# Bias network recorded in text order ahead of the null key and value, its norm's factor moved into later steps

## The chip, the cores and the metric

The kernel runs on one core of a Trainium2 chip, in one launch. A core has five instruction streams that work side by side and wait for each other through semaphores: TensorE (PE, matmul and transpose), VectorE (DVE), ScalarE (ACT), GpSimd (POOL) and SyncE (SP, which issues DMAs); ACT issues some DMAs too. Each stream takes its instructions in the order in which they stand. The metric is the device time of the program in microseconds (us); less is better. Times in the trace are counted from the start of its span.

## The reference, cut to what matters

A batch of 8 sequences of 512 tokens and 256 channels goes through a conditioned attention, a delta-rule mixer and two mixtures of experts, all in float32. The change lies in what is prepared once for the attention: the relative position bias, and the part of the keys and values that belongs to the null key.

```python
def rel_pos_bias(n, w0, b0, g0, w1, b1, g1, w2, b2, dtype):
    pos = jnp.arange(-n + 1, n, dtype=dtype)[:, None]
    h = jax.nn.silu(ln(pos @ w0 + b0, g0))
    h = jax.nn.silu(ln(h @ w1 + b1, g1))
    h = h @ w2 + b2
    ...
    bias = h[idx]                       # idx = i - j + n - 1, one value for each head and distance
    return jnp.transpose(bias, (2, 0, 1))
```

Here `ln` subtracts the mean, divides by the root of variance plus 1e-5 and multiplies by a gain. The network has two hidden layers of 256 channels and ends in 16 heads. Attention is causal, so 512 positions are enough. The null key and value are one more column of the scores: `cond[0]` and `cond[1]`, the key normed and scaled by q_scale and k_scale.

## The kernel before, in words

`attention_setup` (from L142) loads the weights, runs the bias network, prepares the null key and value, and spreads the bias. After it comes one long order of steps (`attention_plan`, from L595): a row of score groups, and with every other piece of work due at a step number (`at(w.first - 14, attention_keys, s)`). `a.run(end)` records all steps up to `end`. Setup calls it three times: `a.run(-27)` (the first load of x), `a.run(-4)` after the null key (statistics, norm, turn, keys and queries of the first sequence), and the rest after setup.

The order on an engine is set by two things. Instructions recorded through `Ordered` or `a.mm` and `a.turn` keep the order of the program among themselves; those called straight on `nc` are placed by a scheduler that may move them past others. Before the change, SP's DMAs, the planned steps on DVE and ACT, and matmuls and turns of the plan keep program order; the whole setup calls `nc` directly and is woven between them, and POOL is free throughout.

The bias network works on four tiles of 128 positions. `act_T` (L208) is its step for one tile: mean and variance (`bn_stats` as_nst, `bn_aggr` as_nmv), plus eps, power -0.5 on POOL (as_nr, L101), subtract and multiply (L114), multiply by the gain (L211), tanh of half (L213), (tanh + 1) times h (L214), two turns on TensorE (as_tp, L217) and a copy from PSUM with factor 0.5 (as_h1T, as_h2T, L218). The first layer's h is position times w0 plus b0 (L224), the second's a matmul with w1 (as_hp, L229) plus b1 (L233). The last matmul with w2 gives as_gp (L237), DVE makes as_gs of it (L240), and SP writes it to DRAM as as_gd.

The null key: as_nrow and as_rk on DVE, a power on POOL, then for each of two halves as_wn on POOL (L257) and a sum on DVE into a_wkv's last 16 columns (L263). a_kp, the matmul of the keys (L131), reads a_wkv. The null value: as_nvb is cleared on POOL (L279) and filled by two copies on DVE (L280, L281), and eight matmuls with Wout make as_vps (L284), which is copied to a_vw.

Spreading the bias: for each of the 16 heads a DMA (half of them issued by SP, half by ACT) reads as_gd with shifted rows into as_hk (four buffers), one matmul with a flipped identity, called a flip here, makes as_bp (L274, two PSUM buffers), and ACT copies it into a_bias (L275). The first score group's a_bm (L450, POOL: bias plus mask row) reuses the room of setup's tiles, and so waits until they have been read.

The planned steps that lie beside this for the first sequence: statistics of x (a_st, a_mv), the norm's factors on POOL (a_nr, a_nmr), the mask row (a_mrow, L342), norm on ACT (a_x), turns (a_tp) and their copies (a_xnT), keys (a_kp, a_kv, a_k, a_rk, a_kn), their turn (a_ktp), then four half tiles of queries (a_qp, a_q, a_rq, a_sn on POOL, a_qtp). A matmul in float32 shows as two rows in the trace (two passes).

Of the kernel before, what the change touches and what calls it, by code (L numbers as in the profile page):

```python
# [18 lines left out]
P = 128  # L19
B, S, D = 8, 512, 256  # L20
NT = S // P
NCT = D // P
H1, DH = 16, 64
# [3 lines left out]
BIG = 1.0e30  # L27
# [114 lines left out]
def attention_setup(g, ctx, asides):  # L142
# [16 lines left out]
    with tc.tile_pool(name="as_c", bufs=1) as sp, tc.tile_pool(name="as_w", bufs=2) as wk, tc.tile_pool(  # L159
        name="as_ps", bufs=2, space=PSUM  # L160
    ) as ps:

        rows = {}
        for name in ("w0", "b0", "g0"):
            rows[name] = sp.tile([P, D], F32, name="as_" + name)
            src = ins["c_" + name]
            row_bc(a, rows[name], src[0] if name == "w0" else src)
        w1 = sp.tile([P, NCT, D], F32, name="as_w1")
        nc.scalar.dma_start(out=w1, in_=ins["c_w1"].rearrange(by_k, p=P))
        for name in ("b1", "g1"):  # L170
            rows[name] = sp.tile([P, D], F32, name="as_" + name)
            row_bc(a, rows[name], ins["c_" + name])
        w2 = sp.tile([P, NCT, H1], F32, name="as_w2")
        nc.scalar.dma_start(out=w2, in_=ins["c_w2"].rearrange(by_k, p=P))
        attention_plan(g, a, asides)
        a.run(-27)
        a.wkv = wp.tile([P, NCT, KVW], F32, name="a_wkv")
        a.sync.dma_start(out=a.wkv[:, :, 0 : 2 * DH], in_=ins["c_Wkv"].rearrange(by_k, p=P))
        a.wq = wp.tile([P, NCT, H1 * DH], F32, name="a_wq")
        a.sync.dma_start(out=a.wq, in_=ins["c_Wq"].rearrange(by_k, p=P))  # L180
        nrow = sp.tile([P, 4, DH], F32, name="as_nrow")
        row_bc(a, nrow[:, 0, :], ins["cond"][0])
        row_bc(a, nrow[:, 1, :], ins["c_q_scale"])
        row_bc(a, nrow[:, 2, :], ins["c_k_scale"])
        a.gn = wp.tile([P, NCT], F32, name="a_gn")
        nc.scalar.dma_start(out=a.gn, in_=ins["c_g_norm"].rearrange("(c p) -> p c", p=P))
        sc = sp.tile([P, 2], F32, name="as_sc")
        for i in range(2):
            hs = slice(i * DH, (i + 1) * DH)
            a.sync.dma_start(out=sc[hs, 0:1], in_=ins["c_q_scale"].unsqueeze(1))  # L190
            a.sync.dma_start(out=sc[hs, 1:2], in_=ins["c_k_scale"].unsqueeze(1))
        b2 = sp.tile([H1, 1], F32, name="as_b2")
        a.sync.dma_start(out=b2, in_=ins["c_b2"].unsqueeze(1))
        a.nab = wp.tile([P, H1], F32, name="a_nab")
        row_bc(a, a.nab, ins["c_null_attn_bias"])
        a.wout = wp.tile([P, 8, D], F32, name="a_wout")
        nc.scalar.dma_start(out=a.wout, in_=ins["c_Wout"].rearrange(by_k, p=P))
        nv = sp.tile([P, 1], F32, name="as_nv")
        a.sync.dma_start(out=nv[0:DH], in_=ins["cond"][1].unsqueeze(1))
        a.sync.dma_start(out=nv[DH:P], in_=ins["cond"][1].unsqueeze(1))  # L200
        a.go = wp.tile([P, NCT], F32, name="a_go")
        a.sync.dma_start(out=a.go, in_=ins["c_g_out"].rearrange("(c p) -> p c", p=P))


        h1T = sp.tile([P, NCT, S], F32, name="as_h1T")
        h2T = sp.tile([P, NCT, S], F32, name="as_h2T")

        def act_T(out, t, h, gain):  # L208
            hn = wk.tile([P, D], F32, tag="hn", name="as_hn")
            normalized(g, wk, hn, h, "as_n")  # L210
            nc.vector.tensor_mul(hn, hn, gain)  # L211
            th = wk.tile([P, D], F32, tag="th", name="as_th")
            nc.scalar.activation(th, hn, AF.Tanh, scale=0.5)  # L213
            nc.vector.scalar_tensor_tensor(hn, th, 1.0, hn, ALU.add, ALU.mult)  # L214
            tp = ps.tile([P, 512], F32, tag="tp", name="as_tp")
            for c in range(NCT):
                nc.tensor.transpose(tp[:, c * P : (c + 1) * P], hn[:, c * P : (c + 1) * P], g.ident)  # L217
            nc.scalar.activation(  # L218
                out[:, :, t * P : (t + 1) * P], tp[:, 0 : NCT * P].rearrange("p (c m) -> p c m", c=NCT), AF.Copy, scale=0.5
            )  # L220

        for t in range(NT):
            h = wk.tile([P, D], F32, tag="h", name="as_h")
            nc.vector.scalar_tensor_tensor(h, rows["w0"], g.pos[:, t : t + 1], rows["b0"], ALU.mult, ALU.add)  # L224
            act_T(h1T, t, h, rows["g0"])
        for t in range(NT):
            hp = ps.tile([P, 512], F32, tag="ps", name="as_hp")
            for c in range(NCT):
                nc.tensor.matmul(  # L229
                    hp[:, 0:D], h1T[:, c, t * P : (t + 1) * P], w1[:, c, :], start=c == 0, stop=c == NCT - 1  # L230
                )
            h = wk.tile([P, D], F32, tag="h", name="as_h2")
            nc.vector.tensor_add(h, hp[:, 0:D], rows["b1"])  # L233
            act_T(h2T, t, h, rows["g1"])
        gp = ps.tile([P, 512], F32, tag="ps", name="as_gp")
        for c in range(NCT):
            nc.tensor.matmul(gp[0:H1, :], w2[:, c, :], h2T[:, c, :], start=c == 0, stop=c == NCT - 1)  # L237
        gs = sp.tile([H1, S + P], F32, name="as_gs")
        nc.gpsimd.memset(gs[:, S:], BIG)
        nc.vector.tensor_scalar(gs[:, 0:S], gp[0:H1, :], b2, -1.0, ALU.add, ALU.mult)  # L240
        gd = g.dram.tile([H1, S + P], F32, name="as_gd")
        a.sync.dma_start(out=gd, in_=gs)


        nc.vector.tensor_scalar(a.ks, sc[:, 0:1], sc[:, 1:2], -8.0, ALU.mult, ALU.mult)

        rk = sp.tile([P, 1], F32, name="as_rk")
        nc.vector.tensor_mul(nrow[:, 3, :], nrow[:, 0, :], nrow[:, 0, :])
        nc.vector.tensor_reduce(rk, nrow[:, 3, :], AX.X, ALU.add)
        nc.vector.tensor_scalar(rk, rk, 1e-24, None, ALU.max)  # L250
        rsqrt(g, rk, rk)
        nc.vector.tensor_mul(nrow[:, 3, :], nrow[:, 1, :], nrow[:, 2, :])
        nc.vector.tensor_mul(nrow[:, 3, :], nrow[:, 3, :], nrow[:, 0, :])
        nc.vector.tensor_scalar(nrow[:, 3, :], nrow[:, 3, :], rk, -8.0, ALU.mult, ALU.mult)
        wn = sp.tile([P, H1, DH], F32, name="as_wn")
        for c in range(NCT):
            nc.gpsimd.tensor_tensor(  # L257
                wn,
                a.wq[:, c, :].rearrange("p (h d) -> p h d", h=H1),
                nrow[:, 3, :].unsqueeze(1).to_broadcast([P, H1, DH]),  # L260
                ALU.mult,
            )
            nc.vector.tensor_reduce(a.wkv[:, c, 2 * DH : KVW], wn, AX.X, ALU.add)  # L263

        a.run(-4)


        for h in range(H1):
            hk = wk.tile([P, S], F32, tag="hk", name="as_hk", bufs=4)
            row = gd[h]  # L270
            eng = a.sync if h % 2 else nc.scalar
            eng.dma_start(out=hk, in_=bass.AP(tensor=row.tensor, offset=row.offset, ap=[[1, P], [1, S]]))
            bp = ps.tile([P, 512], F32, tag="tp", name="as_bp")
            nc.tensor.matmul(bp, g.flip, hk, start=True, stop=True)  # L274
            nc.scalar.copy(a.bias[:, h, :], bp)  # L275


        nvb = sp.tile([P, 8 * H1], F32, name="as_nvb")
        nc.gpsimd.memset(nvb, 0.0)  # L279
        nc.vector.tensor_copy(nvb[0:DH, 0 : 8 * H1 : H1 + 2], nv[0:DH, 0:1].to_broadcast([DH, 8]))  # L280
        nc.vector.tensor_copy(nvb[DH:P, 1 : 8 * H1 : H1 + 2], nv[DH:P, 0:1].to_broadcast([DH, 8]))  # L281
        vps = ps.tile([P, 512], F32, tag="ps", name="as_vps")
        for c in range(8):
            nc.tensor.matmul(  # L284
                vps[0:H1, 0:D], nvb[:, c * H1 : (c + 1) * H1], a.wout[:, c, :], start=c == 0, stop=c == 7
            )
        nc.vector.tensor_copy(a.vw, vps[0:H1, 0:D])

    a.pp = ctx.enter_context(tc.tile_pool(name="a_pp", bufs=4))
    a.tr = ctx.enter_context(tc.tile_pool(name="a_tr", bufs=2, space=PSUM))  # L290
    a.av = ctx.enter_context(tc.tile_pool(name="a_av", bufs=2, space=PSUM))
# [1736 lines left out]
```

## Time and profile before

| | us |
|---|---|
| three runs: median (lowest, highest) | 2495.55 (2490.47, 2503.61) |
| the profiled execution, whole | 2498.42 |
| its span in the profile | 2496.6 |
| busy in the span: PE, DVE, ACT, POOL | 2336.8, 1422.1, 970.2, 1129.5 |
| bias network: first h, as_gp, as_gs | 7.64, 40.38, 44.01 |
| null key: first as_nrow, last a_wkv over | 19.02, 35.78 |
| the first a_kp, the other seven | 46.46, 47.44 |
| as_vps, the null value's matmuls | 44.70 to 51.68 |
| first and last flip (as_bp) | 52.65, 85.08 over |
| first a_bm | 85.16 |

The last lines are starts in the trace unless they say otherwise. The whole setup is the first 85 us of 2497. A row of the timeline gives start, length (of a merged row: from the first start to the last end), engine, line, operation, output and inputs, and in brackets how long the engine was idle before it and what ended that. The chain of waits is followed back from the last instruction of the span; its rows give start, length, and what the time went to.

### The profile page before, as it was taken

Reading aid. Unit: us, or ns where it says so; the run is one execution under the profiler, and the core shown is the slowest. Engines: PE = TensorE matmul, PEld = TensorE weight load, DVE = VectorE, ACT = ScalarE, POOL = GpSimd, SP = SyncE. Lnnn points to the kernel's source line nnn. Section 1 sums busy time; section 2 is a strip of 40 time slices with the busy share of each in tenths; the row PEclk is TensorE's granted clock in tenths of the full one; section 3 lists DMA queues with packets and bytes.
Section 4 is the critical chain, followed back from the end, with each engine's and each line's share of the span. In section 5 each row is a group of like instructions: output and inputs, shape, how many; then the busy total and the mean of one; then the engine's idle time right before and its main releaser. Section 6 shows DMA issues by size and latency. Waiting matters only on the chain.

```text
span 2496.6 us, 57237 instructions
## 1 busy us (share of the span) xinstructions
PE 2336.8 (94%) x22836; PEld 1726.3 (69%) x22836; DVE 1422.1 (57%) x3974; ACT 970.2 (39%) x2650; POOL 1129.5 (45%) x1427
## 2 busy tenths in 40 slices
PE   4899999999999995779899999999999999999998
PEld 2456565556655653456778787887887888888886
DVE  4466657676675775445647457466466467444333
ACT  2666767566666652322222223223222322211111
POOL 3677867767787651333324324225224234232211
PEclk7999999999999997768999999999999999999999
DMA  3201012011110014011323323334225134232433
GB/s 99 60 19 39 28 36 59 22 37 40 35 32 27 23 52 117 2 31 49 78 74 100 83 77 104 77 84 117 66 79 122 50 95 112 72 108 76 115 95 88
DMA packets 345179, 167.25 MB, mean 67 GB/s; under 512 B 193280, under 2 KB 323072, under 8 KB 344912
## 3 DMA queue, kind: packets, MB, share of 16 engines
q1 hardware_dynamic: 341904, 160.16, 23.9%
q8 instruction: 180, 2.95, 0.5%
q10 hardware_dynamic: 3008, 3.43, 0.5%
q14 instruction: 87, 0.71, 0.1%
HBM read 148.33 MB, written 15.18 MB: 65 GB/s over the span
## 4 chain that ended last, share of the span: by engine, by line
PE 76%; DVE 11%; POOL 5%; DMA 3%; ACT 2%; issue 2%; SPq 1%; ACTq 0%; DVEq 0%; POOLq 0%
PE m_guf L131 13%; PE m_gue L131 9%; PE m_accf L131 6%; PE a_op L131 6%; PE a_s L131 5%; PE a_av L131 4%; PE a_qp L131 4%; PE m_acce L131 4%; PE a_ptp L132 4%; PE d_pp L131 3%; PE d_op L131 2%; PE m_lp L131 2%; POOL a_bm L450 1%; DVE d_y L125 1%; PE d_cop L131 1%
## 5 line engine op out<-in xcount | busy, mean ns | idle before, releaser
L450 POOL TENSOR_TENSOR a_bm<-a_bias,a_mrow 128x1024 f32<-128x1024 f32 (+1 forms) x176 | 381.9, 2171 | 81.6 <-DVE a_mn L125 69.0
L131 PE MATMUL m_guf<-m_oute,m_wf 128*128 128x256 f32 x1536 | 379.8, 392 | 3.2 <-ACT m_oute L125 2.0
L131 PEld LDWEIGHTS m_guf<-m_oute,m_wf 128*128 128x128 f32 x1536 | 292.2, 195 | 56.3 <-issue 8.4
L131 PE MATMUL m_gue<-m_xT,m_we 128*128 128x256 f32 x1280 | 311.5, 386 | 11.4 <-DVE m_he L125 10.1
L125 DVE CUSTOM_DVE_ANT_0 a_pr<-a_s,a_bm,a_sn 128x512 f32<-128x512 f32 (+3 forms) x512 | 254.4, 546 | 66.1 <-PE a_s L131 51.0
L125 ACT ACTIVATE a_pr<-a_pr,a_mn 128x512 f32<-128x512 f32 (+3 forms) x512 | 282.0, 553 | 16.3 <-DVE a_mn L125 15.6
L131 PEld LDWEIGHTS m_gue<-m_xT,m_we 128*128 128x128 f32 x1280 | 236.8, 191 | 49.0 <-DVE m_he L125 14.2
L125 POOL TENSOR_TENSOR m_hf<-m_hf,m_ctf 128x256 f32<-128x256 f32 x128 | 97.0, 759 | 381.7 <-DVE m_hf L125 211.7
L125 DVE SCALAR_TENSOR_TENSOR m_tf<-m_tf,m_guf 128x256 f32<-128x256 f32 x192 | 80.5, 419 | 301.2 <-ACT m_tf L125 300.8
L125 ACT ACTIVATE m_tf<-m_guf 128x256 f32<-128x256 f32 x192 | 73.5, 383 | 373.9 <-PE m_guf L131 369.5
L125 POOL TENSOR_TENSOR m_he<-m_he,m_cte 128x256 f32<-128x256 f32 x128 | 105.1, 821 | 223.7 <-DVE m_he L125 121.1
L131 PE MATMUL a_s<-a_kT,a_qT 64*128 64x384 f32 (+3 forms) x1024 | 199.8, 471 | 6.7 <-DVE a_mn L125 6.4
L131 PE MATMUL m_accf<-m_hf,m_wf 128*128 128x256 f32 x768 | 200.1, 384 | 6.0 <-POOL m_hf L125 6.0
L125 DVE TENSOR_TENSOR m_te<-m_gue,m_te 128x256 f32<-128x256 f32 x160 | 67.7, 423 | 230.2 <-ACT m_te L125 230.2
L132 PE MATMUL a_ptp<-table,a_pr 128*128 128x128 f32 x1280 | 179.6, 278 | 19.7 <-DVE a_pT L125 18.2
L132 PEld LDWEIGHTS a_ptp<-table,a_pr 128*128 128x128 f32 x1280 | 145.5, 142 | 76.0 <-issue 29.5
L125 ACT ACTIVATE m_te<-m_gue 128x256 f32<-128x256 f32 x160 | 61.3, 383 | 290.8 <-PE m_gue L131 276.9
L131 PE MATMUL a_av<-a_pT,a_kv 128*64 128x256 f32 (+1 forms) x1216 | 165.1, 402 | 3.1 <-DVE a_pT L125 3.0
L131 PEld LDWEIGHTS m_accf<-m_hf,m_wf 128*128 128x128 f32 x768 | 148.1, 193 | 28.0 <-POOL m_hf L125 7.2
L131 PE MATMUL m_acce<-m_he,m_we 128*128 128x256 f32 x640 | 163.8, 381 | 0.0
L131 PEld LDWEIGHTS a_s<-a_kT,a_qT 64*128 64x128 f32 x1024 | 83.6, 186 | 80.1 <-issue 39.9
L131 PEld LDWEIGHTS m_acce<-m_he,m_we 128*128 128x128 f32 x640 | 121.6, 191 | 17.0
(350 smaller groups left out, 4169.2 us busy)
## 6 DMA issues: line engine op xcount, KB each, us to landing
a_rep<-a_rd SPq DMA_DIRECT2D x128, 128.0 KB
m_cte<-m_combe SPq DMA_DIRECT2D x64, 256.0 KB
m_ctf<-m_combf SPq DMA_DIRECT2D x128, 128.0 KB
m_we<-in_e_w_gate_dram SPq DMA_DIRECT2D x64, 128.0 KB
m_we<-in_e_w_up_dram SPq DMA_DIRECT2D x64, 128.0 KB
m_we<-in_e_w_down_dram SPq DMA_DIRECT2D x64, 128.0 KB
m_wf<-in_f_gate_w_dram SPq DMA_DIRECT2D x128, 64.0 KB
m_wf<-in_f_up_w_dram SPq DMA_DIRECT2D x128, 64.0 KB
```

The costliest lines, as they stand in the source:

```text
L125: return lambda *args, **kw: tc.keep_in_program_order(f(*args, **kw))
L131: mm = lambda *args, **kw: tc.keep_in_program_order(pe.matmul(*args, **kw))
L132: turn = lambda *args: tc.keep_in_program_order(pe.transpose(*args))
L450: nc.gpsimd.tensor_tensor(bm, a.bias[:, 2 * c0 : 2 * (c0 + pairs), (NT - 1 - t) * P :], s.mrow[:, 0:n].unsqueeze(1).to_broadcast([P, 2 * p ...
```

## The change

The network is recorded in text order. POOL is wrapped in `Ordered` for the length of setup, and DVE, ACT and TensorE use the plan's ordered handles; the null key's and null value's POOL and DVE instructions do the same (as_vps and the flips still call `nc`). The network stands first, then `a.run(-16)`, which records the first sequence's statistics, norm and turn, then the null key, then `a.run(-4)`. The memsets of as_gs and as_nvb, which the scheduler had put at the start of POOL's order, now stand where the text has them.

Within the network the work of a tile is cut into `first`/`second`, `centred` and `silu`, recorded a piece apart for neighbouring tiles. The norm's factor r is no longer multiplied into h. POOL makes x.r from 4 times the variance plus 4e-5, so x.r is half the old factor; tanh takes it as its scale; the first layer's output goes without it through w1 and gets it in the second layer's bias step (y.r); the second layer's output gets it in a copy on ACT (`last`). For each tile and layer the step for eps and one of two passes over h on DVE are gone, and POOL has one small instruction more. In all, DVE has 16 instructions fewer in the changed program, POOL 8 more and ACT 4 more.

In the changed program's order on TensorE, as_vps is split: two of its eight matmuls stand between the seventh and the eighth flip, two between later flips, and four behind the last one, ahead of the first scores. The load of ACT's function table waits for the first `centred` tile; before it waited for nothing. From the second score group on, every engine's order is that of before.

```diff
+        a.nc.gpsimd = Ordered(tc, nc.gpsimd)
+        v, act, pool = a.nc.vector, a.nc.scalar, a.nc.gpsimd
...
+        def summed(x, gain):
+            x.gain = gain
+            st = wk.tile([P, 6], F32, tag="as_nst", name="as_nst", bufs=4)
+            v.bn_stats(st, x.h)
+            x.mv = wk.tile([P, 2], F32, tag="as_nmv", name="as_nmv", bufs=4)
+            v.bn_aggr(x.mv, st)
+            x.r = wk.tile([P, 1], F32, tag="as_nr", name="as_nr", bufs=8)
+            pool.tensor_scalar(x.r, x.mv[:, 1:2], 4.0, 4e-5, ALU.mult, ALU.add)
+            pool.tensor_tensor(x.r, x.r, g.nhalf, ALU.pow)
+
+        def first(t):
+            x = layers[0][t]
+            x.h = wk.tile([P, D], F32, tag="h", name="as_h", bufs=4)
+            v.scalar_tensor_tensor(x.h, rows["w0"], g.pos[:, t : t + 1], rows["b0"], ALU.mult, ALU.add)
+            summed(x, rows["g0"])
+
+        def second(t):
+            y, x = layers[0][t], layers[1][t]
+            hp = ps.tile([P, 512], F32, tag="ps", name="as_hp")
+            for c in range(NCT):
+                a.mm(hp[:, 0:D], h1T[:, c, t * P : (t + 1) * P], w1[:, c, :], start=c == 0, stop=c == NCT - 1)
+            x.h = wk.tile([P, D], F32, tag="h", name="as_h2", bufs=4)
+            v.scalar_tensor_tensor(x.h, hp[:, 0:D], y.r, rows["b1"], ALU.mult, ALU.add)
+            summed(x, rows["g1"])
+
+        def centred(x):
+            v.scalar_tensor_tensor(x.h, x.h, x.mv[:, 0:1], x.gain, ALU.subtract, ALU.mult)
+            x.th = wk.tile([P, D], F32, tag="th", name="as_th", bufs=2)
+            act.activation(x.th, x.h, AF.Tanh, scale=x.r)
+
+        def silu(x, out, last):
+            v.scalar_tensor_tensor(x.h, x.th, 1.0, x.h, ALU.add, ALU.mult)
+            if last:
+                act.activation(x.h, x.h, AF.Copy, scale=x.r)
             tp = ps.tile([P, 512], F32, tag="tp", name="as_tp")
             for c in range(NCT):
-                nc.tensor.transpose(tp[:, c * P : (c + 1) * P], hn[:, c * P : (c + 1) * P], g.ident)
-            nc.scalar.activation(
-                out[:, :, t * P : (t + 1) * P], tp[:, 0 : NCT * P].rearrange("p (c m) -> p c m", c=NCT), AF.Copy, scale=0.5
-            )
+                a.turn(tp[:, c * P : (c + 1) * P], x.h[:, c * P : (c + 1) * P], g.ident)
+            act.copy(out[:, :, x.t * P : (x.t + 1) * P], tp[:, 0 : NCT * P].rearrange("p (c m) -> p c m", c=NCT))
 
         for t in range(NT):
...
+            first(t)
+        for t in range(NT + 1):
+            if t < NT:
+                centred(layers[0][t])
+            if t > 0:
+                silu(layers[0][t - 1], h1T, False)
+        for t in range(NT + 2):
+            if t < NT:
+                second(t)
+            if 0 < t <= NT:
+                centred(layers[1][t - 1])
+            if t > 1:
+                silu(layers[1][t - 2], h2T, True)
         gp = ps.tile([P, 512], F32, tag="ps", name="as_gp")
...
-        nc.gpsimd.memset(gs[:, S:], BIG)
-        nc.vector.tensor_scalar(gs[:, 0:S], gp[0:H1, :], b2, -1.0, ALU.add, ALU.mult)
+        pool.memset(gs[:, S:], BIG)
+        v.tensor_scalar(gs[:, 0:S], gp[0:H1, :], b2, -1.0, ALU.add, ALU.mult)
         gd = g.dram.tile([H1, S + P], F32, name="as_gd")
         a.sync.dma_start(out=gd, in_=gs)
+        a.run(-16)
...
-        rsqrt(g, rk, rk)
+        pool.tensor_tensor(rk, rk, g.nhalf, ALU.pow)
...
         for c in range(NCT):
-            nc.gpsimd.tensor_tensor(
+            pool.tensor_tensor(
                 wn,
...
-            nc.vector.tensor_reduce(a.wkv[:, c, 2 * DH : KVW], wn, AX.X, ALU.add)
+            v.tensor_reduce(a.wkv[:, c, 2 * DH : KVW], wn, AX.X, ALU.add)
 
         a.run(-4)
...
         nvb = sp.tile([P, 8 * H1], F32, name="as_nvb")
-        nc.gpsimd.memset(nvb, 0.0)
-        nc.vector.tensor_copy(nvb[0:DH, 0 : 8 * H1 : H1 + 2], nv[0:DH, 0:1].to_broadcast([DH, 8]))
-        nc.vector.tensor_copy(nvb[DH:P, 1 : 8 * H1 : H1 + 2], nv[DH:P, 0:1].to_broadcast([DH, 8]))
+        pool.memset(nvb, 0.0)
+        v.tensor_copy(nvb[0:DH, 0 : 8 * H1 : H1 + 2], nv[0:DH, 0:1].to_broadcast([DH, 8]))
+        v.tensor_copy(nvb[DH:P, 1 : 8 * H1 : H1 + 2], nv[DH:P, 0:1].to_broadcast([DH, 8]))
...
+    a.nc.gpsimd = nc.gpsimd
```

More of the change, by code (lines that the diff above doesn't have):

```diff
@@ L202, in attention_setup @@
         a.sync.dma_start(out=a.go, in_=ins["c_g_out"].rearrange("(c p) -> p c", p=P))
+        a.nc.gpsimd = Ordered(tc, nc.gpsimd)
+        v, act, pool = a.nc.vector, a.nc.scalar, a.nc.gpsimd
         h1T = sp.tile([P, NCT, S], F32, name="as_h1T")
         h2T = sp.tile([P, NCT, S], F32, name="as_h2T")
[L208 to L214, printed above, removed]
+        layers = [[SimpleNamespace(t=t) for t in range(NT)] for _ in range(2)]
@@ L222, in attention_setup @@
         for t in range(NT):
[L223 to L234, printed above, removed]
+            first(t)
@@ L235, in attention_setup @@
+        for t in range(NT + 1):
[10 more added lines that the diff above has]
+                silu(layers[1][t - 2], h2T, True)
         gp = ps.tile([P, 512], F32, tag="ps", name="as_gp")
         for c in range(NCT):
-            nc.tensor.matmul(gp[0:H1, :], w2[:, c, :], h2T[:, c, :], start=c == 0, stop=c == NCT - 1)
+            a.mm(gp[0:H1, :], w2[:, c, :], h2T[:, c, :], start=c == 0, stop=c == NCT - 1)
@@ L238, in attention_setup @@
         gs = sp.tile([H1, S + P], F32, name="as_gs")
-        nc.gpsimd.memset(gs[:, S:], BIG)
-        nc.vector.tensor_scalar(gs[:, 0:S], gp[0:H1, :], b2, -1.0, ALU.add, ALU.mult)
+        pool.memset(gs[:, S:], BIG)
+        v.tensor_scalar(gs[:, 0:S], gp[0:H1, :], b2, -1.0, ALU.add, ALU.mult)
         gd = g.dram.tile([H1, S + P], F32, name="as_gd")
         a.sync.dma_start(out=gd, in_=gs)
-        nc.vector.tensor_scalar(a.ks, sc[:, 0:1], sc[:, 1:2], -8.0, ALU.mult, ALU.mult)
+        a.run(-16)
@@ L247, in attention_setup @@
+        v.tensor_scalar(a.ks, sc[:, 0:1], sc[:, 1:2], -8.0, ALU.mult, ALU.mult)
         rk = sp.tile([P, 1], F32, name="as_rk")
-        nc.vector.tensor_mul(nrow[:, 3, :], nrow[:, 0, :], nrow[:, 0, :])
-        nc.vector.tensor_reduce(rk, nrow[:, 3, :], AX.X, ALU.add)
-        nc.vector.tensor_scalar(rk, rk, 1e-24, None, ALU.max)
-        rsqrt(g, rk, rk)
-        nc.vector.tensor_mul(nrow[:, 3, :], nrow[:, 1, :], nrow[:, 2, :])
-        nc.vector.tensor_mul(nrow[:, 3, :], nrow[:, 3, :], nrow[:, 0, :])
@@ L254, in attention_setup @@
-        nc.vector.tensor_scalar(nrow[:, 3, :], nrow[:, 3, :], rk, -8.0, ALU.mult, ALU.mult)
+        v.tensor_mul(nrow[:, 3, :], nrow[:, 0, :], nrow[:, 0, :])
+        v.tensor_reduce(rk, nrow[:, 3, :], AX.X, ALU.add)
+        v.tensor_scalar(rk, rk, 1e-24, None, ALU.max)
+        pool.tensor_tensor(rk, rk, g.nhalf, ALU.pow)
+        v.tensor_mul(nrow[:, 3, :], nrow[:, 1, :], nrow[:, 2, :])
+        v.tensor_mul(nrow[:, 3, :], nrow[:, 3, :], nrow[:, 0, :])
+        v.tensor_scalar(nrow[:, 3, :], nrow[:, 3, :], rk, -8.0, ALU.mult, ALU.mult)
@@ L286, in attention_setup @@
             )
-        nc.vector.tensor_copy(a.vw, vps[0:H1, 0:D])
+        v.tensor_copy(a.vw, vps[0:H1, 0:D])
+    a.nc.gpsimd = nc.gpsimd
     a.pp = ctx.enter_context(tc.tile_pool(name="a_pp", bufs=4))
```

## The prediction

> **What bounds the kernel now.** The page gives TensorE 94% of the span, but the change touches only the setup, so I read the chain of waits over the first 140 us, then the timeline of that stretch, then the windows table for the clock. The chain:
>
> ```profile
> 40.38 3.59 PE as_gp L237 x4
> ...
> 55.79 1.11 PE a_ktp L132 x4
> 56.90 9.31 PE a_qp L131 x16
> ...
> 68.72 2.68 PE as_bp L274 x6
> 71.42 3.81 DMA as_hk<-as_gd
> ...
> 85.16 6.99 POOL a_bm L450 x3
> ```
>
> The end of setup is one event, POOL's first a_bm at 85.16. The timeline says what it waited for, and gives the rows that I use below (start, length, engine, instruction, idle time before and its releaser):
>
> ```profile
> 23.07 2.40 POOL L257 TENSOR_TENSOR as_wn<-a_wq,as_nrow 128x1024 f32<-128x1024 f32 x1 [2.39 <-DVE as_nrow L254]
> ...
> 34.59 1.19 DVE L263 TENSOR_REDUCE a_wkv<-as_wn 128x16 f32<-128x1024 f32 x1
> ...
> 44.01 0.74 DVE L240 TENSOR_SCALAR as_gs<-as_gp,as_b 16x512 f32<-16x512 f32 x1 [4.29 <-PE as_gp L237]
> ...
> 47.44 1.98 PE L131 MATMUL a_kp<-a_wkv,a_xnT 128*128 128x144 f32 x14
> ...
> 52.54 1.93 POOL L342 TENSOR_SCALAR a_mrow<-a_mk 128x512 f32<-128x512 uint8 x1
> ```
> ```profile
> 73.41 0.22 POOL L422 TENSOR_TENSOR a_sn<-a_sn,a_nab 128x16 f32<-128x16 f32 x1
> ...
> 85.16 6.99 POOL L450 TENSOR_TENSOR a_bm<-a_bias,a_mrow 128x1024 f32<-128x1024 f32 x3 [11.54 <-PE as_bp L274]
> ```
>
> The reader is to see that a_bm waits for the sixteenth flip (as_bp), not for arithmetic; that the null key's work (as_wn, a_wkv) was over by 35.8, inside the network's gaps; and that a_kp started at 47.44 because its inputs were long there. The second of the two fences above shows POOL's q work over at 73.63, after which POOL idled 11.54.
>
> **What the change does to the order.** In the changed program every engine's order is the same as before from the second score group on, to the last instruction. So the change can only move the time of the first a_bm; what it moves, the whole rest follows. Counts: DVE loses 16 instructions (per tile and layer the eps step, 0.15, and one of the two 0.41 passes), POOL gains 8 (times 4 plus 4e-5), ACT gains 4 (a copy by r). The loads are issued in the old order.
>
> *Step 1, the network: as_gp from 40.4 to 35.0.* DVE starts at 7.64, as before. Four tiles of h, statistics, aggregate at 0.46 + 0.49 + 0.10 end at 11.84; centred 0.42. The ACT table load (1.28, at 2.80 before, hidden) now stands behind a wait for the first centred tile: on the path, 12.3 to 13.6. Tanh 0.42 to 14.0; then silu 0.42, turn 0.72, copy 0.39, with the next tanh behind each copy on ACT (0.73 a tile): the last turn starts at 17.3, the first as_hp at 17.75. Before, the chain stood 6.53 at the cond load (DVE's as_nrow L248 queued in the middle of the network); that stall goes, since as_nrow now comes after the network. Layer two: as_hp 2.0 a tile at the clock seen then; h from tile 0 at 19.8, 1 at 21.5, 2 at 23.2. The fourth as_hp is queued on TensorE behind tile 0's turn, which waits for centred, tanh, silu and the new copy (25.6): 26.1 to 28.0. From there 0.46 + 0.49 + 0.10, centred, two silu and the copies on ACT, where each tanh or copy by r takes turns with a 0.39 copy: tile 3's silu ends at 32.4, its copy by r at 33.75, turn and copy at 34.9. as_gp 34.95, as_gs 3.63 later at 38.6 (44.0 before): 5.4 earlier. Not in the trace: tanh and copy with a factor per partition. Bounds are the plain tanh, 0.42, and a_x's activation with two such factors, 0.59; I take 0.42, the high end adds some 0.5. The small POOL step goes by a_nr's 0.25.
>
> *Step 2, the null key: a_kp from 47.4 to 54.8.* DVE's statistics of x0, which filled gaps before, are now queued behind as_gs: 4 x 0.59 from 39.25, the last aggregate done at 41.7. POOL then runs in text order: a_nr to a_nmr 1.96 (39.81 to 41.77 before), a_mrow 1.94, rk's power 0.6 (45.7 to 46.3), DVE as_nrow 0.3, as_wn 2.4 (to 49.05), the second a_mrow 1.94 (to 51.0), as_wn 2.45 (to 53.5), DVE a_wkv 1.19: 54.75. The first of eight a_kp runs at 50.4, when the first a_wkv is there, and flip 1 behind it; the second a_kp waits for 54.75, and the other six and flips 2 to 4 are queued behind it. xnT would have let it start at 47.6. This chain of 10.1 us on POOL was hidden in the network; now nothing covers it.
>
> *Step 3, keys: +5.3.* From a_kp to a_ktp before 8.35 (47.44 to 55.79), of which 2.0 was the second a_mrow in POOL's way, now already done: 54.8 + 6.3 = 61.1.
>
> *Step 4, queries: +5.3.* Same instructions, same waits: POOL's a_sn ends at 73.6 + 5.3 = 79.0. Only then comes the memset of as_nvb (0.19; at 0.87 before), then DVE's two copies (0.17 each). The 1.99 of the first copy before lies over as_wn (27.8 to 30.2) and isn't repeated, as POOL then only waits. as_vps can start at 79.6.
>
> *Step 5, the new wait.* as_vps stands on TensorE in front of flip 8 of 16, and TensorE takes its queue in order: nine flips, four of them already loaded, wait for it; a_bias, SP's and ACT's loads of as_hk and a_bm wait for them. Before, as_vps was done by 51.7. Price: two as_vps (4 passes) 0.9, nine flips at the old cadence (flip 5's a_bias copy at 71.42 to the last at 85.12: 11 in 13.7, 1.25 each, set by four buffers and the 3.81 load) 11.2, then four as_vps (8 passes of 0.23, from ten in 2.33) 1.9: a_bm at **93.6**. Bounds of the flips: 0.92 each where the loads lag nowhere (3.0 less), 1.7 at half clock.
>
> *Behind a_bm.* TensorE has the first scores (1.2), a turn and a_qp (2.5) still to do, done before already; exp starts some 1.8 later against a_bm. ACT has idle stretches of 0.85 (at 92.34) and 2.24 (at 100.21) there, and POOL is the chain until 102.6, so I cost this at nothing; without that cover 0.9.
>
> **Sum.** 93.6 - 85.2 = +8.4 us, 0.34%. The profiled execution took 2498.4 (span 2496.6): 2506.8 on its account; it lies 2.9 above the median of the three times, so against the median 2495.55 + 8.4 = **2504**.
>
> **The clock.** The windows table (stretch, its length, busy time of PE, PEld, DVE, ACT and POOL, granted clock, DMA):
>
> ```profile
> 52.00:56.00 4.00, 1.31 (x3) 0.51 (x4) 0.13 (x1) 0.58 (x1) 3.57 (x4) 0.85 0.11 43
> 56.00:60.00 4.00, 4.00 (x8) 2.04 (x8) 0.00 (x0) 0.69 (x1) 0.00 (x0) 0.50 0.26 66
> ```
>
> After a stretch with TensorE mostly idle the clock is 0.50, and a_qp's passes take 0.85 instead of 0.43 until 61.4. The changed order makes two such gaps: 46.8 to 54.8 (ahead of a_kp) and about 75 to 79.6 (ahead of as_vps). The Trainium skill ("TensorE: Matmul & The Clock Gate", Part 1) states that an idle window of about 3.4 us halves the clock and a busy window of that length restores it. By it both restarts would be at half clock; as an estimate from its window, 1.5 more at a_kp and 1 more at the flips, +10.9 in all. The sum above does not use it.
>
> **Rivals.**
> 1. *Half clock at both restarts, slower by over 0.5%.* By this trace's rows the slow stretch lasts 5.6 (55.8 to 61.4): a_kp's 14 passes 1.98 more at most, the first flips 1.7 instead of 1.25 (three or four of them, 1.6), as_vps in front 0.8, 8.4 + 4.4 = +12.8, and +13.3 with the high end of step 1: 2495.55 + 13.3 = 2509. It decides from 12.5 on. Against it: a_kp cold makes a_qp warm (6.9 instead of 9.3), which gives back up to 2.4. 17%.
> 2. *The shorter network is what counts.* If the null key were hidden as before, the old times shift by 5.4: 2490. For it: 5.4 at as_gs. Against it: POOL's order, as_wn behind a_nr and a_mrow, leaves no way. 5%.
> 3. *The change doesn't carry:* the late a_bm is caught up behind it, within 3 us of before: 2496. Against it: POOL has no gap from 85.16 to 105.5. 6%.
> Forecast, +3 to +12.5: 72%.
>
> **Range and chances.** Low: flips at 0.92 and a quicker network, +3.5; high: the network saves nothing, +13.8. The three times before lie 13 apart, so a median may be off by 3 or so: 2496 to 2513. Half a per cent is 12.5 us, about what a measurement here can tell from no change. Rival 1 and the upper edge of the forecast give slower 0.22; faster by that much only with a stray time, 0.03; the rest 0.75.
>
> **What would show it.** The table load near 12.3 with tanh behind it; as_gs near 38.6; a_kp in two parts, the second after a_wkv near 54.8; a_ktp near 61; flips 8 to 16 after 80, POOL idle ahead of a_bm for over 13 us; a_bm released by as_vps near 93.6; the rest the same. Wrong if a_bm starts before 85, or if as_vps does not stand in front of the flips.

## The result, and the profile after

| | before | after |
|---|---|---|
| median (lowest, highest) of ten executions each, us | 2493.16 (2486.87, 2503.61) | 2509.85 (2502.71, 2516.69) |
| profiled execution, its span, us | 2498.42, 2496.6 | 2514.58, 2512.8 |
| as_gp, as_gs | 40.38, 44.01 | 34.94, 38.57 |
| last a_wkv over, second a_kp | 35.78, 47.44 | 54.64, 54.79 |
| a_ktp, last a_sn over | 55.79, 73.63 | 62.84, 77.67 |
| as_vps, first row to last | 44.70 to 51.68 | 78.36 to 93.88 |
| first a_bm | 85.16 | 94.11 |

The changed kernel is slower: the ratio of the times is 1.0048, with a 95% interval of 1.0031 to 1.0066 (the two medians alone give 1.0067). Up to the first a_bm the setup became 8.95 us longer, where 8.4 was forecast.

The chain of waits of the changed kernel over its setup (start, length, engine, what, line):

```profile
34.94 3.61 PE as_gp L131 x4
38.57 0.75 DVE as_gs L125
...
43.55 1.93 POOL a_mrow L125
...
46.49 2.40 POOL as_wn L125
...
48.98 1.93 POOL a_mrow L375
...
50.98 2.42 POOL as_wn L125
53.42 1.23 DVE a_wkv L125
...
54.79 3.71 PE a_kp L131 x14
...
62.84 0.66 PE a_ktp L132 x4
...
77.45 0.22 POOL a_sn L125
77.67 0.15 POOL as_nvb L125
...
78.36 1.86 PE as_vps L316 x4
80.22 3.73 PE as_bp L306 x4
83.98 4.05 DMA as_hk<-as_gd
...
88.17 3.88 PE as_bp L306 x8
92.05 1.84 PE as_vps L316 x8
...
94.11 7.00 POOL a_bm L483 x3
```

In the chain of before, as_wn and a_wkv lay inside the network (23.07 to 35.16 of that chain) and as_vps among the turns and a_kp (44.76 to 47.51); nothing of the null key stood behind as_gp and nothing of the null value behind the second a_kp. Now the null key lies between as_gs and a_kp, and the null value between a_sn and the flips. as_gp starts 5.4 earlier. From there to the second a_kp it is 19.85 for 7.06, 12.8 more, and from a_kp to a_bm 39.32 for 37.72, 1.6 more: together +8.95.

The timeline of the changed kernel has three rows that the prediction named (start, length, engine, instruction, in brackets the idle time before it and its releaser):

```profile
12.07 1.28 ACT L125 ACT_TABLE_LOAD   x1 [12.07 <-DVE as_h L125]
...
63.33 7.03 PE L131 MATMUL a_qp<-a_wq,a_xnT 128*128 128x512 f32 x16
...
94.11 7.00 POOL L483 TENSOR_TENSOR a_bm<-a_bias,a_mrow 128x1024 f32<-128x1024 f32 x3 [16.30 <-PE as_vps L316]
```

The table load waits for the first centred tile, a_qp takes 7.03 for 9.51 in the timeline of before, and POOL idles 16.30 for 11.54 ahead of a_bm, now released by as_vps. The windows table of the changed kernel says at what clock a_kp and the flips behind as_vps ran (columns as in the prediction; the granted clock is the third number from the end):

```profile
56.00:60.00 4.00, 4.00 (x14) 2.97 (x13) 0.35 (x1) 0.80 (x2) 0.61 (x1) 0.50 0.00 0
60.00:64.00 4.00, 3.16 (x11) 1.46 (x10) 0.07 (x1) 2.22 (x4) 2.46 (x4) 0.98 0.56 164
...
76.00:80.00 4.00, 1.64 (x4) 0.43 (x4) 1.03 (x3) 0.00 (x0) 1.66 (x4) 0.66 0.25 81
80.00:84.00 4.00, 4.00 (x6) 1.75 (x6) 0.00 (x0) 0.61 (x2) 0.00 (x0) 0.50 0.07 25
```

Both a_kp and the first flips behind as_vps ran at half clock. For a_kp this is no new fall of the clock: it stands at 0.50 in every window from 28 to 60. a_qp was spared: TensorE had been busy from 54.79 to 62.0, with a_kp and three flips, and the clock was back (0.98 over 60 to 64).

**Behind a_bm.** The ends of the same instructions in both traces give the shift along the run: +8.95 at a_bm, +8.96 at 160, +8.7 at the last a_pr (944), +9.1 at the first m_he (1160). There it is still the setup's. Then it wanders: +11.0 at the first m_ob (1375), +10.5 at the eighth (1912), +16.3 at the end. These last 7 us are the subject of the first experiment.

### The profile page after: what moved, and what is told of

Its sections match the earlier page's. It is cut to its first block, busy times and chain, and to the rows that moved or that the text cites. A ratio compares the mean times of both kernels' runs of the same rounds, so it can differ in the third digit from the quotient of the medians.

```text
span 2512.8 us, 57231 instructions
## 1 busy us (share of the span) xinstructions
PE 2347.8 (93%) x22836; PEld 1733.9 (69%) x22836; DVE 1418.4 (56%) x3958; ACT 972.2 (39%) x2654; POOL 1131.1 (45%) x1435
## 4 chain that ended last, share of the span: by engine, by line
PE 76%; DVE 11%; POOL 5%; DMA 3%; ACT 2%; issue 2%; SPq 1%; POOLq 0%; DVEq 0%; ACTq 0%
PE m_guf L131 14%; PE m_gue L131 9%; PE m_accf L131 6%; PE a_op L131 5%; PE a_s L131 5%; PE a_av L131 5%; PE m_acce L131 4%; PE a_ptp L132 4%; PE a_qp L131 4%; PE d_pp L131 3%; PE d_op L131 2%; PE m_lp L131 2%; POOL a_bm L483 1%; PE d_cop L131 1%; PE d_uwp L131 1%
## 5 line engine op out<-in xcount | busy, mean ns | idle before, releaser
L131 PE MATMUL m_gue<-m_xT,m_we 128*128 128x256 f32 x1280 | 312.5, 387 | 10.3 <-DVE m_he L125 9.4
```

The source lines that it names most:

```text
L131: mm = lambda *args, **kw: tc.keep_in_program_order(pe.matmul(*args, **kw))
```

## The experiments

The theory was that of the prediction: the order of the null key and the null value puts two chains ahead of a_bm, and the whole run follows a_bm. The rivals were that the new network arithmetic, or the clock of the later stages, makes the difference. All kernels in a table; the time of each is the median of 12 executions (after 10, old_network_early 9, early_eight_loads 6), and the ratio is against 10 to 35 executions of before, its own for each batch (it isn't the quotient of two medians). The starts are those of one trace each:

| kernel | as_gs | second a_kp | a_sn over | first a_bm | median us | ratio to before (95%) |
|---|---|---|---|---|---|---|
| before_again | 44.61 | 47.93 | 74.06 | 85.99 | 2500.33 | 1.0011 (0.9991 to 1.0031) |
| after | 38.57 | 54.79 | 77.67 | 94.11 | 2509.85 | 1.0048 (1.0031 to 1.0066) |
| old_network | 33.38 | 49.59 | 72.46 | 88.10 | 2504.66 | 1.0029 (1.0008 to 1.0049) |
| key_early | 39.12 | 48.29 | 70.56 | 85.98 | 2500.03 | 0.9996 (0.9976 to 1.0017) |
| value_early | 38.84 | 55.06 | 77.93 | 86.29 | 2503.70 | 1.0016 (0.9998 to 1.0033) |
| key_value_early | 37.51 | 46.68 | 69.56 | 79.24 | 2496.50 | 0.9987 (0.9969 to 1.0005) |
| value_late_alone | 43.81 | 45.93 | 70.65 | 86.59 | 2504.41 | 1.0016 (1.0001 to 1.0032) |
| network_mended | 34.95 | 51.05 | 73.92 | 89.20 | 2506.13 | 1.0022 (1.0002 to 1.0042) |
| table_early | 35.79 | 51.90 | 74.78 | 90.27 | 2504.46 | 1.0019 (0.9999 to 1.0039) |
| old_network_early | 33.25 | 40.41 | 61.76 | 70.73 | 2485.16 | 0.9941 (0.9920 to 0.9961) |
| early_eight_loads | 33.48 | 40.61 | 61.98 | 69.31 | 2480.57 | 0.9914 (0.9893 to 0.9934) |

A straight line through the eleven ratios against the first a_bm rises by 0.00049 per us, that is 1.2 us of time for one of a_bm, with a correlation of 0.97. No kernel lies more than 3.3 us off it. Without the last two rows, which lie far from the others, it is 1.0 us for one (correlation 0.91), so a shift that is carried 1 to 1 fits as well.

### before_again: the kernel before once more

> The kernel before, unchanged, run again for the granted clock and span of each of its runs. Main theory (the change costs what it adds ahead of the first a_bm, about 9 us, and what lies above that in the profiled pair is a scatter of the clock that both kernels have): the runs of before scatter by 10 us or more, the slow ones at a lower mean clock, and at equal clock before is 8 to 9 shorter than the changed kernel (whose runs went from 2502.7 at 0.959 to 2516.7 at 0.953). Rival (the change itself lowers the clock later on): all runs of before lie at 0.957 or above and within 5 us.

The twelve executions went from 2490.27 to 2509.32, at clocks of 0.963 to 0.958: the scatter of the main theory, four times what the rival allowed. The 35 executions of before that ran beside this batch of four kernels went from 2480.06 to 2510.36. Ten executions are few against that: before had medians of 2493.2, 2496.7, 2500.3 and 2501.2 on four occasions, so the 16.7 between the two medians above is partly a low reading of before. The line through all kernels gives 10.5 from an a_bm of 85.5 to one of 94.11, and 8.6 without the last two rows.

The comparison at equal clock did not come out: at 0.959 three executions of before_again took 2500.35 to 2503.09 and the changed kernel 2502.71; at 0.958 three took 2503.05 to 2509.32 and two of the changed kernel 2504.08 and 2504.90. That is no difference, where 8 to 9 was expected. But the mean clock is no independent measure here, as the longer setup itself lowers it: over the first 100 us the granted clock was 0.86 and 0.90 in the two traces of before and 0.80 in that of the changed kernel. That is 0.0024 to 0.004 of the whole run's mean, and 0.001 goes with some 2.2 us within one kernel's executions, so by an estimate 5 to 9 us are hidden by comparing so.

What the last 7 us are: the two traces of the *same* program before differ by 0.3 at the last a_pr, by 9.6 at the first m_he and by 5.9 at the end. In the last stages single stretches run at half clock while TensorE is full, in other places in each execution. Windows of before around one such stretch, and of the changed kernel around the same work:

```profile
1317.00:1321.20 4.20, 4.20 (x32) 3.93 (x30) 3.81 (x7) 0.25 (x1) 1.59 (x4) 1.00 0.34 81
1321.20:1324.60 3.40, 3.40 (x10) 2.75 (x10) 2.47 (x9) 0.23 (x1) 0.00 (x0) 0.50 0.05 15
```
```profile
1326.00:1330.00 4.00, 4.00 (x29) 3.70 (x28) 3.19 (x6) 0.38 (x1) 1.59 (x4) 0.99 0.25 57
1330.00:1333.40 3.40, 3.40 (x11) 2.99 (x12) 3.09 (x10) 0.23 (x1) 0.00 (x0) 0.50 0.18 49
1333.40:1336.80 3.40, 3.40 (x10) 2.21 (x11) 1.25 (x3) 0.90 (x2) 0.28 (x1) 0.50 0.00 0
```

TensorE is busy for the whole of each window, and the clock is 0.50 for one window of 3.4 in before and for two in the changed kernel. From 1240 to 2480 the clock's records in the two traces show 30.7 us of this before and 44.4 after; 13.7 us more at half clock is up to 6.8 lost, and the shift grows by 6.6 there (9.2 to 15.8). That the change makes this more frequent isn't shown: the trace of before_again has 37.5 over the same stretch, and those of the nine kernels below 30.2 to 58.0, the most in value_early, whose a_bm is 7.8 earlier than the changed kernel's. That it has no part in it isn't shown either.

### old_network: the network's arithmetic of before in the new order

In the changed kernel, the code from `layers` to the two loops is replaced by `act_T` and the loops of before, called on `nc`; the rest stays.

> The order of the changed kernel (null key and null value behind the network, POOL in text order) with the network's arithmetic of before, placed by the scheduler. Main theory (the order of the null key and null value is the whole loss; the shorter network comes from the stall that went, not from the factor's place): as_gs within 1.5 us of 38.6, the second part of a_kp within 1.5 of 54.8, first a_bm 92.5 to 95.5, time within 2 us of the changed kernel. Rival (the factor's new place made the network shorter): as_gs near 44, a_bm near 99, time 5 us above the changed kernel.

Neither expectation held. as_gs came at 33.38, 5.2 *earlier* than with the new network. The chain of waits of old_network, with its rows for the start of the network's matmuls:

```profile
13.98 0.39 ACT as_h1T L221
14.42 2.07 PE as_hp L232 x4
...
30.04 3.31 PE as_gp L131 x4
33.38 0.75 DVE as_gs L125
```

The first as_hp starts at 14.42 and as_gp at 30.04; in the changed kernel they start at 17.62 and 34.94. So the step from 40.38 to 34.94 is two terms: some 10.3 gained by the order, and 4.9 lost by the new network. Behind the 10.3 are the wait for the cond load (6.53 in the chain of before), which no longer stands in the network, and the null key's as_wn and a_wkv (2.70 and 1.60 in that chain); no run parts the two. Three differences stand in the rows. The table load is back at 2.79, behind nothing. The scheduler's order takes two tiles through the first layer before it starts the others, so that the second layer begins 3.2 earlier. And tanh takes 0.42 where the one with a factor per partition takes 0.51, with no copy by r behind it. Behind as_gs the order is that of the changed kernel, shifted: a_kp at 49.59 is 5.2 earlier, a_bm at 88.10 is 6.0 earlier, as its as_vps in front took 1.20 for 1.86. The ratio is 1.0029.

### key_early: the null key back in the network's gaps

```diff
+            if t == 3:
+                null_key_row()
             if t < NT:
                 second(t)
+            if t == 3:
+                for c in range(NCT):
+                    null_key_part(c)
...
+        for c in range(NCT):
+            v.tensor_reduce(a.wkv[:, c, 2 * DH : KVW], wn[c], AX.X, ALU.add)
...
         a.run(-16)
-        v.tensor_scalar(a.ks, sc[:, 0:1], sc[:, 1:2], -8.0, ALU.mult, ALU.mult)
...
```

`null_key_row` holds the DVE steps and the power, `null_key_part` one as_wn, each now in a buffer of its own.

> The changed kernel with one part undone: the null key's row is recorded ahead of the fourth second-layer tile, its two as_wn behind it, its sums ahead of as_gs, so that it lies in the network's gaps on POOL and DVE. Main theory: as_gs stays within 1 of 38.6; a_kp runs in one piece near 47.6 instead of 54.8; all behind it 7 earlier: a_sn over near 70.5, the wait for as_vps still there, first a_bm near 87; time 7 below the changed kernel, +2 against before. Rival (the wait of as_vps and the flips' loads set the end, not the keys): a_bm stays above 91 and the time moves by less than 3.

The chain of waits of key_early from as_gs on:

```profile
39.12 0.74 DVE as_gs L125
...
47.51 0.77 PE a_kp L131 x2
48.29 3.13 PE a_kp L131 x14
...
55.76 0.66 PE a_ktp L132 x4
...
70.56 0.15 POOL as_nvb L125
...
71.25 1.01 PE as_vps L323 x2
```

The null key is gone from the chain. a_kp runs in one piece, its last 14 passes from 48.29, a_sn is over at 70.56 as expected, and as_vps still follows it. a_bm is 8.1 earlier, at 85.98 where 87 was expected, and the ratio to before is 0.9996 (0.9976 to 1.0017), where +2 us, 1.0008, was expected. The rival falls. a_kp is slow here too (its 14 passes take 3.13 for the 1.98 of before), though it follows the turns without a gap: the clock is 0.50 in every window from 32 to 48, and comes back within the next one.

```profile
48.00:52.00 4.00, 4.00 (x18) 3.33 (x17) 0.00 (x0) 1.03 (x3) 0.11 (x2) 0.67 0.29 66
```

### value_early: the null value back behind as_gp

```diff
         nvb = sp.tile([P, 8 * H1], F32, name="as_nvb")
-        pool.memset(nvb, 0.0)
+        nc.gpsimd.memset(nvb, 0.0)
```

These two lines move to the start of the network, and the two copies on DVE to the end of it, ahead of `gp`.

> The changed kernel with the other part undone: as_nvb is cleared at the start and filled ahead of as_gs, so that as_vps runs right behind as_gp; the null key stays late. Main theory (as_vps in front of the eighth flip is a wait of its own): a_sn over near 77.7 as in the changed kernel, first a_bm 11.6 behind it as before, near 89.3; time 4.8 below the changed kernel. Rival (the flips are bound by their loads, and the wait only hides that): a_bm at 92 or later, time within 2 us of the changed kernel.

a_sn was over at 77.93, as in the changed kernel, but a_bm came at 86.29, not 89.3: the wait costs 7.8, not 4.8. The end of its chain of waits, and its windows over the flips:

```profile
80.42 1.07 PE as_bp L310 x2
...
81.51 3.47 DMA as_hk<-as_gd
...
85.11 1.11 PE as_bp L310 x2
...
86.29 7.00 POOL a_bm L483 x3
```
```profile
76.00:80.00 4.00, 4.00 (x11) 1.34 (x9) 1.01 (x2) 1.75 (x3) 1.78 (x3) 1.00 0.75 215
80.00:84.00 4.00, 4.00 (x14) 1.79 (x14) 0.00 (x0) 1.87 (x4) 0.00 (x0) 1.00 0.72 218
```

Where the changed kernel has a clock of 0.66 and 0.50, here it is 1.00, and TensorE is full from 76. Three things follow from the one wait: the flips stand still until 78.36, then start cold, and their loads stand still with them, as each needs a buffer that a flip sets free. What is left at the end is one load, 3.47, ahead of the last flip. The rival, by which the loads bind in any case, falls too: they bound the end here, but 7.8 us earlier.

### key_value_early: both

> The changed kernel with both parts undone, as in key_early and value_early together. Main theory (two separate waits, each 7.8 to 8.1 us at the first a_bm, one behind the other): a_kp near 48.3 as in key_early, a_sn over near 70.6, first a_bm 8.4 behind it as in value_early, near 79; time 6 us below before. Rival (each of the two hides the other, and the loads of the flips take over): first a_bm at 83 or later, time that of before.

a_bm came at 79.24, 14.9 before that of the changed kernel; the two prices by themselves add up to 15.9. So they are separate waits, one behind the other, and hide each other by 1 only. The ratio is 0.9987, 3 us below before where 6 were expected; the interval (0.9969 to 1.0005) holds both 6 below and no change.

### value_late_alone: before with only the null value late

```diff
+        a.nc.gpsimd = Ordered(tc, nc.gpsimd)
...
-        nc.gpsimd.memset(nvb, 0.0)
+        a.nc.gpsimd.memset(nvb, 0.0)
```

and the same for the two copies on DVE.

> The kernel before with one part of the change: POOL in program order and as_nvb cleared and filled behind the planned steps, so that as_vps waits among the flips; network and null key as before. Main theory (the wait of as_vps alone costs some 4.5, since before had 11.5 from a_sn to a_bm and the changed kernel 16.4): a_sn over near 74, first a_bm near 90, time 4.5 above before. Rival (the wait costs only where the keys are late too): first a_bm within 1.5 of 85.5, time as before.

a_bm came at 86.59, not 90, only 0.6 to 1.4 later than in the two traces of before. This is the number of the rival (within 1.5 of 85.5), but not for its reason, as the wait itself is there: from a_sn's end to a_bm it is 15.9, against 11.5 to 11.9 before. But a_sn was over 3.0 to 3.4 earlier, at 70.65. as_vps no longer stood on TensorE among the turns and a_kp, whose rows end at 47.92 for 49.42, and a_qp took 7.44 for 9.51. Moving as_vps late gives 3 ahead of a_sn and takes 4.4 behind it. The expectation had counted only the second. The ratio, 1.0016, is not told apart from that of before_again, 1.0011.

### network_mended and table_early: what the new network loses

```diff
+        warm = sp.tile([P, 1], F32, name="as_warm")
+        nc.vector.memset(warm, 0.0)
+        act.activation(warm, warm, AF.Tanh)
...
         second(2)
         centred(layers[1][1])
+        second(3)
         silu(layers[1][0], h2T, True)
         centred(layers[1][2])
-        second(3)
```

network_mended has both parts (the loop over the second layer is written out), table_early the first three lines alone.

> The changed kernel with two edits in its network, arithmetic the same: a tanh of one column at the start takes the table load off the path, and the fourth as_hp is recorded ahead of tile 0's second-layer turn. By old_network the rewritten network is 5.2 slower (as_gs 38.6 against 33.4) than the old one free of its stall. If the table load (1.3) and the queued as_hp (2.7 idle on TensorE) make most of that: as_gs 34.5 to 35.5, first a_bm near 90.5, time 3 to 4 below the changed kernel. If the copies by r on ScalarE and the tile order make it: as_gs above 37, time within 1.5 of the changed kernel.

> The changed kernel with one edit: a tanh of one column at the start, so that the table load does not stand behind the first centred tile. network_mended had this and the moved as_hp, and as_gs at 34.95 against 38.57. If the two parts are worth what they idle: as_gs 1.3 earlier, 37.3, first a_bm near 93 (with the 0.4 that DVE's start scatters), time 1 below the changed kernel. Rival (the load is caught up behind the first as_hp, and the queued as_hp is all of it): as_gs within 0.4 of 38.6.

network_mended gave what it should, as_gs at 34.95. But the table load alone gave 2.8 of these 3.6 (35.79), not 1.3, and the queued as_hp 0.8, not 2.7. So the sizes of table_early's expectation failed (as_gs 37.3, a_bm near 93; it was 90.27), and its rival, as_gs near 38.6, as well. Of the 5.2 between the changed kernel and old_network 1.6 are left, for the slower tanh, the copies by r and the tile order together. The timeline of table_early:

```profile
2.79 1.28 ACT L125 ACT_TABLE_LOAD   x1 [2.79 <-issue]
...
16.23 3.93 PE L131 MATMUL as_hp<-as_w,as_h1T 128*128 128x256 f32 x12
...
23.74 1.03 PE L131 MATMUL as_hp<-as_w,as_h1T 128*128 128x256 f32 x4
```

and the same matmuls in the timeline of the changed kernel:

```profile
17.62 5.25 PE L131 MATMUL as_hp<-as_w,as_h1T 128*128 128x256 f32 x12
...
25.85 1.71 PE L131 MATMUL as_hp<-as_w,as_h1T 128*128 128x256 f32 x4
```

The load is back at 2.79, and the matmuls start 1.4 earlier. The rest is that they are faster: 12 passes take 3.93 for 5.25, the last four 1.03 for 1.71 (0.43 a pass, the cold figure, in the changed kernel). So the queued as_hp costs little once it is warm. Why the earlier burst comes to be warm isn't settled by these rows; the moment at which the clock steps up may lie by chance.

### old_network_early and early_eight_loads: a version that beats both

old_network with as_nvb early as in value_early, and x's statistics and the null key's row ahead of `gp`, where DVE is idle; the power and both as_wn then follow a_nmr on POOL, ahead of the mask row:

```diff
+        a.run(-22)
+        null_key_row()
+        v.tensor_copy(nvb[0:DH, 0 : 8 * H1 : H1 + 2], nv[0:DH, 0:1].to_broadcast([DH, 8]))
...
         gp = ps.tile([P, 512], F32, tag="ps", name="as_gp")
...
+        a.hook = null_key
+        a.run(-21)
+        for c in range(NCT):
+            v.tensor_reduce(a.wkv[:, c, 2 * DH : KVW], wn[c], AX.X, ALU.add)
         a.run(-16)
```

`attention_norm` calls `a.hook` ahead of the mask row of the first sequence, and the fourth tile's gain step goes through `v`, so that nothing of this moves up into the network. early_eight_loads has eight as_hk buffers for four besides.

> The old network's arithmetic, with everything off its path: as in old_network, but x's statistics and the null key's row stand right behind the network's last DVE work, as_rk and both as_wn behind a_nmr and ahead of the mask row, and as_vps behind as_gp. Main theory (the end of setup follows a_kp and the flips, and the rest follows 1 to 1): as_gs near 33.5, a_kp near 40, a_sn over near 62, first a_bm 71 to 74, time 11 to 14 below before. Rival (the loads of the flips take over once the keys are early): first a_bm at 78 or later, time no more than 7 below before.

> old_network_early with eight as_hk buffers for four. If the loads bind the flips there (9.0 from a_sn to a_bm for nine flips, TensorE needing 0.9 to 1.0 for one): flips end 1 to 2 earlier, first a_bm 69 to 70, time 1 to 2 below old_network_early, which no measurement here tells from none. Rival (TensorE and ScalarE's copies bind them): first a_bm within 0.5 of 70.7.

Three rows of the timeline of old_network_early:

```profile
34.23 4.78 POOL L125 TENSOR_TENSOR as_wn<-a_wq,as_nrow 128x1024 f32<-128x1024 f32 x2 [1.17 <-DVE as_nrow L125]
...
40.41 1.95 PE L131 MATMUL a_kp<-a_wkv,a_xnT 128*128 128x144 f32 x14 [0.81 <-DVE a_wkv L125]
...
70.73 7.01 POOL L468 TENSOR_TENSOR a_bm<-a_bias,a_mrow 128x1024 f32<-128x1024 f32 x3 [8.98 <-PE as_bp L293]
```

as_gs 33.25, a_kp 40.41, a_sn over at 61.76, a_bm at 70.73: the main theory's numbers, with a_bm 0.3 below its range. a_kp's 14 passes are warm (1.95); as_vps keeps TensorE busy ahead of them, which is the likely reason. The median is 2485.16, ratio 0.9941 (0.9920 to 0.9961), some 15 below before where 11 to 14 were expected. Eight buffers bring a_bm to 69.31, 1.4 earlier, as the loads theory said, with a ratio of 0.9914 (0.9893 to 0.9934). Both intervals lie below 1, so both beat before and the changed kernel; they overlap, so which of the two is the faster isn't shown.

## Why the prediction was right

The forecast of +8.4 at a_bm came out at +8.95, and the time, 2509.85, lies in the range of 2496 to 2513, 5.9 above the 2504 that was named. That the sum came so near at a_bm is in part luck: step 3 was 1.7 too short (6.3 forecast, 8.05 measured), step 4 3.1 too long (17.9, 14.83) and step 5 1.8 too short (14.6, 16.44). By its own steps:

1. *The network, as_gp 34.95 and as_gs 38.6.* 34.94 and 38.57. The table load stood on the path at 12.07 (12.3 forecast). A tanh with a factor per partition was 0.51, where 0.42 was taken from bounds of 0.42 and 0.59; the Trainium skill ("ScalarE: Activation LUTs", What ACT_TABLE_LOAD costs) gives some 0.093 for each such operand, and 0.51 less 0.42 agrees with it. The sum was right, but what it is made of wasn't said: old_network shows 10.3 gained by the order and 4.9 lost by the new network. What the prediction calls a shorter network is a slower one.
2. *The null key, second a_kp 54.8.* 54.79. Reading POOL's order off and adding its rows gave the time to 0.01 (the rows in between lie up to 0.2 off), and key_early shows that this is the cause: without it, a_bm is 8.1 earlier.
3. *Keys, a_ktp 61.1.* 62.84. a_kp took 3.71 for 1.98: the half clock that rival 1 priced and step 3 had left out.
4. *Queries, a_sn over 79.0.* 77.67. a_qp was warm, 7.03 for 9.51. The prediction named this as up to 2.4 in its rival and didn't use it.
5. *The wait of as_vps, a_bm 93.6.* 94.11. The mechanism held, and its parts were a little small: as_vps in front 1.86 for 0.9, as it was cold, the nine flips with two pairs of as_vps between them 11.8 for 11.2, the last as_vps 1.84 for 1.9. The price by itself was mis-sized: the sum put 14.6 from a_sn to a_bm against 11.5 before, 3.1 more; it was 16.4, and value_early shows 8.4 without the wait, so that it costs 7.8. Before was no measure of a run of flips without the wait.
6. *Behind a_bm, 0.* +8.95 at a_bm, +8.7 at the end of the attention: nothing was caught up, and the price of 0.9 without cover wasn't paid.

Rival 1 was half right: a_kp and the flips behind as_vps were at half clock. But its 4.4 were not added up, since a_qp behind the cold a_kp was 2.5 shorter. And the gap that it names ahead of a_kp is not what slowed a_kp: the clock was 0.50 from 28 on, and without the gap, in key_early, it was 0.50 until a_kp was all but over.

Ahead of as_vps TensorE was idle from 74.78 to 78.36, 3.58 us, and the clock fell to 0.50 at 77.3, 2.5 into this gap; in value_early, where the gap is gone, it stays at 1.00. The Trainium skill's rule ("TensorE: Matmul & The Clock Gate", Part 1) that an idle window of about 3.4 us halves the clock gives the same outcome for this gap, but in these traces less idle time was enough: in key_early the whole gap ahead of as_vps was 2.63, and the clock was 0.50 behind it. Nor does the length alone decide: behind 2.64 in value_late_alone the clock stayed at 1.00, and behind 3.59 in table_early it fell only at 76.6, when as_vps had run at full speed (1.02 for 1.86). Windows of the changed kernel, of key_early and of value_late_alone:

```profile
77.40:78.00 0.60, 0.00 (x0) 0.00 (x0) 0.15 (x1) 0.00 (x0) 0.36 (x2) 0.50 0.06 21
```
```profile
72.00:74.00 2.00, 2.00 (x3) 0.50 (x2) 0.00 (x0) 0.00 (x0) 0.00 (x0) 0.50 0.00 0
```
```profile
72.00:74.00 2.00, 2.00 (x6) 0.58 (x7) 0.00 (x0) 0.59 (x1) 0.00 (x0) 1.00 0.04 12
```

Rival 2, the hidden null key, fell. Rival 3, the catching up, fell as well.

What the forecast missed is the step from +8.95 in the setup to the 12 that the ratio gives (0.48% of 2493; its interval, 7.7 to 16.5, holds the 8.4 of the forecast), and to the 16.7 between the medians. Part of it is a low series of before; by the line through the kernels the change is worth 8.6 to 10.5. The rest lies within the scatter of the half-clock stretches in the last stages, which two executions of before show as well. Whether the change has any part in them stays open.

## What to carry to other kernels

A piece of work that a scheduler had woven into another's gaps has a price when it is put into text order: add its rows on the engine where they now queue, one after the other, and add nothing for the gaps, which are no longer there. A matmul whose inputs come late must not stand in front of a queue that feeds loads: the wait stops the matmuls, their buffers and so the loads behind them, and here the matmuls behind the wait ran at half clock as well. And when a rewritten stage looks shorter, run the old stage in the new order as well; here the order was the gain, and the rewriting lost half of it.

## What the runs showed of the hardware

- Single stretches of 3.4 or 6.8 us at half clock occur in the last stages while TensorE is busy in the whole window (the windows tables above); from 1240 to 2480 there are eight of them in the trace of before and nine in that of the changed kernel. A rule that halves the clock after an idle window doesn't explain these, and the measurement stands. The executions of one program scatter by 19 to 30 us in 2500, and with them the mean clock (0.954 to 0.966 over 35 executions of before); how much of this is these stretches isn't shown.
- The granted clock of a profile begins with its first record, at about 22.6 us in the changed kernel's trace. Its windows table shows 1.00 for 16 to 20 in the changed kernel, where as_hp takes 0.43 a pass, and table_early's last four show 0.26. The duration of a pass is the better thermometer there.
- ScalarE's function table was loaded behind the wait of the first instruction that needs it (at 12.07, released by the centred tile). A tanh of one column ahead of everything (0.20) moved the load from 12.07 to 2.79.
